# A tuned long-convolution kernel: the first convolution in nine block products instead of ten

## The chip, the cores and the metric

The kernel runs on one core of one Trainium2 chip. A core has a matrix engine (TensorE, in the profile PE, with its weight loads as PEld), VectorE (DVE), ScalarE (ACT), GpSimd (POOL) and SyncE (SP), which here issues nearly all DMAs. Each engine works through its own instructions in order; semaphores connect them. Matmul results land in PSUM, everything else lies in SBUF. The metric is device time in microseconds (us) of one execution.

## The reference, cut to what matters

There are 4 images of 64 channels, each 256 x 256, in float32. Layer 0 makes two short filters per channel (a small sine network over 256 positions, times a decay), takes their outer product as a 256 x 256 kernel and convolves each image with it causally (written with FFTs), then adds the image times a bias. Since the kernel is an outer product, it is two one-dimensional convolutions, one along each axis.

```python
hx = _implicit_filter(z, Xw1, ..., t, deltas)
hy = _implicit_filter(z, Yw1, ..., t, deltas)
k = jnp.einsum('ijk,imk->ijmk', hx, hy)[0]          # an outer product for each channel
y = jnp.fft.irfft2(u_f * k_f, s=(fft_size, fft_size))[..., :L, :L]
out = y + x * bias[:, None, None]
```

Layer 1 takes, for each image and channel, the 256 x 256 gram matrix of the rows, weighs it with a matrix of the channel, sums each row, adds that sum to the row, and normalises each channel over all images and positions.

```python
scores = jnp.einsum('bpsd,bptd->bpst', x, x) * inv_dim
red = jnp.sum(scores * weights[None], axis=-1, keepdims=True)
y = x + red
mean = jnp.mean(y, axis=(0, 2, 3), keepdims=True)
var = jnp.var(y, axis=(0, 2, 3), keepdims=True)
y_hat = (y - mean) * jax.lax.rsqrt(var + BN_EPS)
return y_hat * gamma[None, :, None, None] + beta[None, :, None, None]
```

## The kernel before, in words

The work goes channel by channel, and all four images of a channel are worked on together: two lie in the upper and lower 64 partitions (called `u`), two behind each other (called `v`). An axis of 256 is cut into 4 blocks of 64. Matmuls are 64 x 64 tiles of the array, so that four run side by side, one for each pair of `u` and `v` (the index `t` of the matmul loops).

Each channel c passes three stages on PE:

- `conv_z(c, m)` (L211), the first convolution. A causal convolution of a 256-vector is a lower triangular Toeplitz matrix, in 4 x 4 blocks of 64 with 10 that aren't zero. Block i of the input (as weights) meets the filter's columns from 64 i on, so the four matmuls are 256, 192, 128 and 64 columns wide. The Toeplitz rows lie in the tile `toep` (`hs[c]`), loaded from `g_dram` by `load_h` in four DMAs and doubled to the lower partitions by `copy_h` on ACT.
- `conv_x0(c)` (L236), the second convolution along the other axis, with the same four widths. It reads `z`, which `copy_z` on ACT has brought from PSUM (L220).
- `gram(c, v)` (L299), the gram matrix; as it is symmetric, only 10 of 16 blocks are made, in matmuls of 192 and 128 columns.

On DVE, `add_bias` (L246) brings the second convolution out of PSUM and adds the image times its bias. `weigh` (L328 `junk`, L319 `pr`) multiplies the gram blocks with the weights; row sums over the free axis come as accumulators, the rest stays as `pr`. `spread` (L340, `sp`) puts the row sums on a diagonal and adds `pr`, so that one sum over all partitions gives `red`: `all_sum` (L348), a partition all-reduce of 1024 columns on POOL. `pick_red` (L357) on ACT moves half of the result, and `add_red` (L364) on DVE adds it to the image and accumulates the sum for the mean. `sum_means` (inside `add_red`, L368) and `sum_squares` (L422) are small all-reduces on POOL; `squares` (L416) on ACT sums the squares; `root` (L428 to L432) on ACT and five small DVE operations (`newton` and `scale_shift`, L437 to L450) give the scale and shift of the channel; `finish` (L462) on ACT writes the output tile, and SP sends it out.

The order is written out by hand (`manual_schedule`): the main loop's body c runs over channels 0 to 61, and `last_channels` holds the last two. In body c, PE does conv_x0(c), then conv_z(c+1), then gram(c). DVE does add_bias(c), the small operations of channel c-3, weigh and spread of the first half of gram(c), then add_red(c-1), then weigh and spread of the second half. POOL gets all_sum(c) at the end of body c, so that its result is used in body c+1. PSUM is a pool of 8 single banks that are handed out in turn.

Of the kernel before, what the change touches and what calls it, by code (L numbers as in the profile page):

```python
# [19 lines left out]
GW = S + P // 2  # L20
COPIES = 4
H = P // 2
# [15 lines left out]
def conv_scores_bn_kernel(  # L38
# [29 lines left out]
    def load_xt(c, v, n):  # L68
        if not n:
            xts[c, v] = ld.tile([P, 4, S], F32, tag=f"xt{v}", name=f"xt_{c}_{v}", bufs=4)  # L70
        part = bass.ts(n, 2)
        nc.sync.dma_start(xts[c, v][:, part], xT[c, v, :, part])
# [39 lines left out]
    g_sb = const.tile([P, GW], F32, name="g_sb")  # L112
    nc.vector.memset(g_sb[:, S:], 0.0)

    g0_sb = const.tile([P, 2, GW], F32, name="g0_sb")
# [3 lines left out]

    g_dram = dram.tile([COPIES, C, 2, GW], F32, name="g_dram")  # L120

    hs[0] = ld.tile([P, 2, GW], F32, tag="toep", name="toep_0")
    with tc.tile_pool(name="fps", bufs=4, space=PSUM) as fps:
# [20 lines left out]
        for a in (1, 0):  # L144
# [7 lines left out]
            for n in range(2):  # L152
                row = g0_sb[H * n : H * n + 1, a, 32 * n :]
                src = bass.AP(row.tensor, row.offset, [row.ap[0], [1, 32], [1, S]])
                queue = nc.scalar if n else nc.sync
                queue.dma_start(hs[0][bass.ts(n, 32), a, :S], src)
# [5 lines left out]
        nc.vector.tensor_tensor(g_sb[:, :S], ph, decay_sb, ALU.mult)  # L162
        for a in (1, 0):
            nc.vector.tensor_copy(hs[0][H:, a, :S], hs[0][:H, a, :S])
# [4 lines left out]
    for a in (1, 0):  # L169
        queue = nc.scalar if a else nc.sync  # L170
        queue.dma_start(
            g_dram[:, :, a, :].rearrange("n c g -> c n g"),
            g_sb[bass.ts(a, C), None, :].to_broadcast([C, COPIES, GW]),
# [4 lines left out]
    def load_h(c, n):  # L178


        if not n:
            hs[c] = ld.tile([P, 2, GW], F32, tag="toep", name=f"toep_{c}")
        src = bass.AP(
            g_dram.tensor, g_dram.offset + c * 2 * GW + 16 * n,
            [[4 + C * 2 * GW, COPIES], [1, 4], [1, GW + S]],
        )
        rows = hs[c][bass.ts(n, 16)].rearrange("p a r -> p (a r)")
        nc.sync.dma_start(rows[:, : GW + S], src)

    def copy_h(c):  # L190

        toep = hs[c]
        nc.scalar.copy(toep[H:, :, :S], toep[:H, :, :S])  # L193
# [3 lines left out]
    ps = ctx.enter_context(tc.tile_pool(name="ps", bufs=8, space=PSUM))  # L197

    st8, zs = {}, {}

    def conv_z(c, m):


        toep = hs[c]
        p1 = [ps.tile([P, 2, S], F32, tag="ps", name=f"p1_{c}_{m}_{u}") for u in range(2)]
        for k in range(2):
            for i in range(4):
                for t in range(4):
# [3 lines left out]
                        p1[u][bass.ts(v, H), k, : S - H * i],  # L212
                        lhsT=xts[c, v][rows, i, bass.ts(2 * m + k, H)],
                        rhs=toep[rows, 1, H * i : S], start=(i == 0), stop=(i == 3),
# [3 lines left out]
    def copy_z(c, m, p1):  # L218
        for u in range(2):
            nc.scalar.copy(zs[c][:, u, bass.ts(m, 2), :], p1[u][:, :, ::-1])  # L220

    def conv_x0(c, z, parts=range(2)):
# [3 lines left out]
        if not c:  # L226
            first_x0(z)
            return
        for m in parts:
            p2 = [ps.tile([P, 2, S], F32, tag="ps", name=f"p2_{c}_{m}_{v}") for v in range(2)]  # L230
            for i in range(2):
                for k in range(4):
                    for t in range(4):
                        v, u = t % 2, t // 2
                        rows = bass.ts(v, H)
                        nc.tensor.matmul(  # L236
                            p2[v][bass.ts(u, H), i, : S - H * k],
                            lhsT=z[rows, u, k, bass.ts(2 * m + i, H)],
                            rhs=toep[rows, 0, H * k : S], start=(k == 0), stop=(k == 3),
                        )  # L240
            add_bias(c, m, p2)

# [539 lines left out]
```

## Time and profile before

| | |
|---|---|
| runs | 885.39, 882.55, 880.49 us |
| median | 882.55 us |
| span of the profiled execution | 872.5 us (its own device time isn't given apart from the span; the median of the runs lies 10 us above the span) |
| busy: PE, DVE, ACT, POOL | 855.9, 755.9, 621.9, 427.8 us |
| DMA | 169.69 MB, mean 194 GB/s |

The span runs from the first to the last instruction of the profiled execution. An engine's busy time counts overlapping instructions once. In the groups and windows, a mean can be longer than the distance from one start to the next, since an engine begins an instruction before the one ahead has ended. A wait is put down to what ended it.

### The profile page before, as it was taken

Reading aid. Unit: us, or ns where it says so; the run is one execution under the profiler, and the core shown is the slowest. Engines: PE = TensorE matmul, PEld = TensorE weight load, DVE = VectorE, ACT = ScalarE, POOL = GpSimd, SP = SyncE. Lnnn points to the kernel's source line nnn. Section 1 sums busy time; section 2 is a strip of 40 time slices with the busy share of each in tenths; the row PEclk is TensorE's granted clock in tenths of the full one; section 3 lists DMA queues with packets and bytes.
Section 4 is the critical chain, followed back from the end, with each engine's and each line's share of the span. In section 5 each row is a group of like instructions: output and inputs, shape, how many; then the busy total and the mean of one; then the engine's idle time right before and its main releaser. Section 6 shows DMA issues by size and latency. Waiting matters only on the chain.

```text
span 872.5 us, 55963 instructions
## 1 busy us (share of the span) xinstructions
PE 855.9 (98%) x24674; PEld 836.2 (96%) x24674; DVE 755.9 (87%) x2647; ACT 621.9 (71%) x1218; POOL 427.8 (49%) x194
## 2 busy tenths in 40 slices
PE   7999999999999999999999999999999999999995
PEld 5999999999999999999999999999999999999994
DVE  3588988988988988988998998998998988988996
ACT  2256767767767767777777777777777767767786
POOL 0236546546546546546546546546546546546530
PEclk9999999999999999999999999999999999999997
DMA  6724665565565556565565565655555655565535
GB/s 189 221 77 139 198 209 195 201 211 193 201 210 192 200 196 206 202 207 193 203 208 192 203 206 194 205 200 199 203 201 199 202 203 192 204 210 193 190 141 194
DMA packets 89870, 169.69 MB, mean 194 GB/s; under 512 B 10555, under 2 KB 11740, under 8 KB 89628
## 3 DMA queue, kind: packets, MB, share of 16 engines
q1 hardware_dynamic: 88972, 165.52, 55.6%
q8 instruction: 194, 3.18, 1.6%
q10 hardware_dynamic: 656, 0.59, 0.3%
q14 instruction: 48, 0.39, 0.2%
HBM read 98.18 MB, written 67.76 MB: 190 GB/s over the span
## 4 chain that ended last, share of the span: by engine, by line
PE 97%; DVE 2%; DMA 1%; issue 0%; ACT 0%; DVEq 0%; ACTq 0%
PE p L211 32%; PE g L299 32%; PE p L236 32%; PE p L265 0%; DMA toep<-g_sb 0%; PE ph L132 0%; DVE junk L328 0%; DMA zw_sb<-in_zw 0%; PE rp L379 0%; DVE fa L135 0%; DVE x L516 0%; DVE pr L319 0%; PE rp L384 0%; PE s L507 0%; DVE fa L140 0%
## 5 line engine op out<-in xcount | busy, mean ns | idle before, releaser
L348 POOL PARTITION_ALL_REDUCE rd<-sp x62 | 376.8, 6078 | 182.4 <-DVE sp L340 182.4
L211 PE MATMUL p<-toep,xt 64*64 64x256 f32 (+3 forms) x8192 | 304.0, 296 | 0.9 <-DMA toep<-g_sb 0.9
L299 PE MATMUL g<-x 64*64 64x192 f32 (+1 forms) x8192 | 302.5, 296 | 0.0
L211 PEld LDWEIGHTS p<-toep,xt 64*64 64x64 f32 x8192 | 291.4, 133 | 8.6 <-PE idle L168 1.5
L236 PE MATMUL p<-toep,z 64*64 64x256 f32 (+3 forms) x8064 | 298.3, 296 | 0.0
L236 PEld LDWEIGHTS p<-toep,z 64*64 64x64 f32 x8064 | 289.6, 133 | 6.8 <-issue 0.2
L299 PEld LDWEIGHTS g<-x 64*64 64x64 f32 x8192 | 289.7, 133 | 0.8 <-DVE x L246 0.2
L328 DVE SCALAR_TENSOR_TENSOR junk<-g,w 128x192 f32<-128x192 f32 x512 | 160.9, 351 | 81.1 <-PE g L299 77.7
L462 ACT ACTIVATE o<-x,sh,g 128x512 f32<-128x512 f32 x252 | 203.3, 810 | 3.0
L246 DVE SCALAR_TENSOR_TENSOR x<-xt,chan_sb,p 128x512 f32<-128x512 f32 x256 | 173.8, 739 | 7.6 <-PE p L265 7.2
L220 ACT COPY z<-p 128x512 f32<-128x512 f32 x256 | 134.7, 576 | 22.3 <-PE p L211 22.3
L416 ACT ACTIVATE sq<-x,mom 128x1024 f32<-128x1024 f32 x127 | 145.2, 1143 | 3.3 <-DVE x L405 1.1
L364 DVE SCALAR_TENSOR_TENSOR x<-x,rd 128x1024 f32<-128x1024 f32 x122 | 144.1, 1218 | 0.0
L340 DVE SCALAR_TENSOR_TENSOR sp<-eye_sb,red,pr 128x128 f32<-128x128 f32 x492 | 139.0, 344 | 0.0
L368 POOL PARTITION_ALL_REDUCE mom<-mom x61 | 24.5, 401 | 231.1 <-DVE x L364 227.1
L357 ACT COPY rd<-rd 64x512 f32<-64x512 f32 (+1 forms) x62 | 38.0, 612 | 134.8 <-POOL rd L348 134.7
L319 DVE SCALAR_TENSOR_TENSOR pr<-g,w 128x256 f32<-128x256 f32 x256 | 107.3, 419 | 0.0
L193 ACT COPY toep<-toep 64x512 f32<-64x512 f32 x63 | 38.9, 617 | 32.0 <-DMA toep<-g_dram 26.7
L411 ACT ACTIVATE mom<-mom 128x1 f32<-128x1 f32 x62 | 18.2, 293 | 38.0 <-POOL mom L368 37.1
L328 DVE DVE_READ_ACCUMULATOR junk<-g,w 128x1 f32 x512 | 42.2, 82 | 0.0
L422 POOL PARTITION_ALL_REDUCE tot<-mom x62 | 29.8, 481 | 5.1 <-ACT sq L416 5.1
L416 ACT ACTIVATION_READ_ACCUMULATOR sq<-x,mom 128x1 f32 x127 | 23.7, 186 | 0.0
(84 smaller groups left out, 220.4 us busy)
## 6 DMA issues: line engine op xcount, KB each, us to landing
xt<-in_xT SPq DMA_DIRECT2D x256, 256.0 KB
out<-o SPq DMA_DIRECT2D x256, 256.0 KB
w<-in_wl SPq DMA_DIRECT2D x64, 320.0 KB
toep<-g_dram SPq DMA_DIRECT2D x252, 36.0 KB
g_dram<-g_sb SPq DMA_DIRECT2D x1, 320.0 KB
g_dram<-g_sb ACTq DMA_DIRECT2D x1, 320.0 KB
decay_sb<-in_decay SPq DMA_DIRECT2D x1, 256.0 KB
fw_sb<-in_fw ACTq DMA_DIRECT2D x1, 192.0 KB
```

Of the source, the lines that this page charges most:

```text
L211: nc.tensor.matmul(p1[u][bass.ts(v, H), k, : S - H * i], lhsT=xts[c, v][rows, i, bass.ts(2 * m + k, H)], rhs=toep[rows, 1, H * i : S], sta ...
L220: nc.scalar.copy(zs[c][:, u, bass.ts(m, 2), :], p1[u][:, :, ::-1])
L236: nc.tensor.matmul(p2[v][bass.ts(u, H), i, : S - H * k], lhsT=z[rows, u, k, bass.ts(2 * m + i, H)], rhs=toep[rows, 0, H * k : S], start=(k ...
L246: nc.vector.scalar_tensor_tensor(st8[c][0][:, v, part], xts[c, v][:, part], chan_sb[:, 0, c : c + 1], p2[v][:, :, ::-1], ALU.mult, ALU.add,)
L299: nc.tensor.matmul(gs[u][bass.ts(h, H), o, :], lhsT=xb[rows, v, i, m, :], rhs=xb[rows, v, i, t, :], start=(i == 0), stop=(i == 3),)
L319: nc.vector.scalar_tensor_tensor(pr[:, b].rearrange("p (t s) -> p t s", s=H), g[:, COL, :], 1.0 / math.sqrt(S), w[:, 6:10, :], ALU.mult, A ...
L328: nc.vector.scalar_tensor_tensor(junk, g[:, part, :], 1.0 / math.sqrt(S), w[:, 3 * n : 3 * n + 3, :], ALU.mult, ALU.mult, accum_out=red0[: ...
L340: nc.vector.scalar_tensor_tensor(sp[:, b, part], eye_sb, red0[:, b, n : n + 1], pr[:, b, part], ALU.mult, ALU.add,)
L348: nc.gpsimd.partition_all_reduce(rd[:, part].rearrange("p b s -> p (b s)"), sp[:, part].rearrange("p b s -> p (b s)"), P, RED.add,)
L364: nc.vector.scalar_tensor_tensor(x0[:, v], x0[:, v], 1.0, rd[:, 2 * v, None, :].to_broadcast([P, 4, S]), ALU.mult, ALU.add, accum_out=mom[ ...
L416: nc.scalar.activation(sq, st8[c][0][:, v], AF.Square, bias=mom[:, 5:6], accum_out=mom[:, 6 + v : 7 + v])
L462: nc.scalar.activation(o, y, AF.Identity, bias=sh, scale=g)
```

## The change: what it does

In rows and columns of blocks, two of the ten products use the same filter block h1: one output takes h1 x1 + h0 x2 and the next h2 x1 + h1 x2, where x1 and x2 are input blocks. The changed kernel computes h1 (x1 + x2) once, and adds (h0 - h1) x2 to the one and (h2 - h1) x1 to the other. The filter differences are made once, at the start, and stored as further columns of `g_dram` (so `toep` has 832 columns instead of 576 that are loaded). The sum x1 + x2 is made by `sums(c + 2)` with two additions of 256 columns on GpSimd, two channels ahead. `conv_shared` makes the shared product with 16 matmuls of 64 columns; ACT copies it to the tile `kept`; `conv_z` makes the other eight blocks (widths 256, 2 x 64, 64, 64); `copy_z` on ACT brings the half of `z` that has no shared part, and `add_shared` on DVE adds `kept` to the other half. Channels 0, 1 and 63 keep the ten products (`conv_z_plain`).

PSUM is now handed out as four pairs of banks. Two `add_bias` of 512 columns become one of 1024 over both banks (in the main loop), and two products `pr` of 256 columns one of 512.

DVE's order in body c is now: add_bias of the first half (c,0); add_red(c-2) in two parts; add_bias(c,1); spread(c-1), eight instructions; add_shared(c+1) twice; weigh of both halves of gram(c). The five small operations of channel c-3 stand one by one between these. Body c issues all_sum(c-1) after the spreads, where body c issued all_sum(c) at its end before. ACT's and SP's orders are moved to fit.

In the order of the changed kernel's instructions, POOL has in each body: the small all-reduce of `sum_squares(c-3)`, that of `sum_means(c-2)`, an entry without operands, the two additions of `sums`, an entry without operands, and the all-reduce of `all_sum(c-1)`. The kernel before has one such entry, ahead of its first `all_sum`.

```diff
     def load_xt(c, v, n):
-        if not n:
-            xts[c, v] = ld.tile([P, 4, S], F32, tag=f"xt{v}", name=f"xt_{c}_{v}", bufs=4)
+        if c not in xts:
+            xts[c] = ld.tile([P, 2, 4, S], F32, tag="xt", name=f"xt_{c}", bufs=4)
...
+        g = g_sb[:, S:]
+        nc.vector.tensor_tensor(g[:, :S], ph, decay_sb, ALU.mult)
+        for n in range(2):
+            nc.vector.tensor_tensor(
+                g_sb[:, bass.ts(n, P)], g[:, (1 + 2 * n) * H :][:, :P], g[:, P:S], ALU.subtract
+            )
...
-        nc.scalar.copy(toep[H:, :, :S], toep[:H, :, :S])
-    ps = ctx.enter_context(tc.tile_pool(name="ps", bufs=8, space=PSUM))
+        nc.scalar.copy(toep[H:], toep[:H])
+    ps = ctx.enter_context(tc.tile_pool(name="ps", bufs=4, space=PSUM))
+    def pair_of_banks(name):
+        return ps.tile([P, 2, 2, S], F32, tag="ps", name=name)
+    def sums(c):
+        xss[c] = wk.tile([P, 2, S], F32, tag="xs", name=f"xs_{c}")
+        for v in range(2):
+            nc.gpsimd.tensor_tensor(
+                xss[c][:, v], xts[c][:, v, 1], xts[c][:, v, 2], ALU.add
+            )
+    def conv_shared(c):
+        toep = hs[c].rearrange("p (b s) -> p b s", s=H)
+        both = ps.tile([P, 2, 8, H], F32, tag="ps", name=f"shared_{c}")
+        for k in range(4):
+            for t in range(4):
+                u, v = t % 2, t // 2
+                rows = bass.ts(u, H)
+                nc.tensor.matmul(
+                    both[bass.ts(v, H), u, k], lhsT=xss[c][rows, v, bass.ts(k, H)],
+                    rhs=toep[rows, 11], start=(k == 0), stop=(k == 3),
+                )
+        kept[c] = wk.tile([P, 2, 2, P], F32, tag="kept", name=f"kept_{c}")
+        nc.scalar.copy(
+            kept[c].rearrange("p m u s -> p u m s"),
+            both[:, :, :4].rearrange("p u (m k) s -> p u m (k s)", k=2),
+        )
     def conv_z(c, m):
...
+        p1 = pair_of_banks(f"p1_{c}_{m}")
+        for k in range(2):
+            for i, (cols, outs) in enumerate((
+                (slice(9, 13), slice(0, 4)),
+                (slice(5, 13, 7), slice(0, 3, 2)),
+                (slice(7, 8), slice(1, 2)),
+                (slice(12, 13), slice(0, 1)),
+            )):
+                for t in range(4):
...
+                    nc.tensor.matmul(
+                        out[:, outs], lhsT=xts[c][rows, v, i, bass.ts(2 * m + k, H)],
+                        rhs=toep[rows, cols], start=(i == 0), stop=(i == 3),
+                    )
+        return p1
     def copy_z(c, m, p1):
-        for u in range(2):
-            nc.scalar.copy(zs[c][:, u, bass.ts(m, 2), :], p1[u][:, :, ::-1])
+        z = zs[c][:, m].rearrange("p u k s -> p (u k) s")
+        y = p1.rearrange("p u k s -> p (u k) s")
+        nc.scalar.copy(z[:, :, :P], y[:, :, : P - 1 : -1])
+    def add_shared(c, m, p1):
+        z = zs[c][:, m].rearrange("p u k (b s) -> p (u k) b s", s=H)
+        y = p1.rearrange("p u k (b s) -> p (u k) b s", s=H)
+        part = kept[c][:, m].rearrange("p u (k s) -> p (u k) s", s=H)
+        nc.vector.tensor_tensor(
+            z[:, :, :1:-1, ::-1], y[:, :, :2],
+            part[:, :, None, :].to_broadcast([P, 4, 2, H]), ALU.add,
+        )
...
+    def weigh_pair(c, v, both):
+        pr, w = st8[c][3], ws[c]
         for u in range(2):
+            weigh_rows(c, 2 * v + u, both[:, u])
+        nc.vector.scalar_tensor_tensor(
+            pr[:, 2 * v : 2 * v + 2].rearrange("p u (t s) -> p u t s", s=H), both[:, :, COL, :],
+            1.0 / math.sqrt(S), w[:, None, 6:10, :].to_broadcast([P, 2, 4, H]),
+            ALU.mult, ALU.mult,
+        )
...
     for c in range(C - 2):
         p, q, f = c - 1, c - 2, c - 3
+        short = c + 1 > 1
...
+        if c:
+            p2 = conv_x0(c, z, 0)
...
+        if c:
+            add_bias(c, 0, p2)
+        if f >= 0:
+            tot = sum_squares(f, moms[f])
+        if q >= 0:
+            pick_red(q)
+        if f >= 0:
+            scales[f] = root(f, tot)
+            steps = scale_steps(f, moms.pop(f), *scales.pop(f))
+        else:
+            steps = iter(())
+        for v in range(2):
+            if q >= 0:
+                add_red(q, v)
+            next(steps, None)
+        if q >= 0:
+            sum_means(moms[q])
+        if c + 2 < C - 1:
+            sums(c + 2)
+        if c:
+            p2 = conv_x0(c, z, 1)
...
+        if c:
+            add_bias(c, 1, p2)
+        if short:
+            conv_shared(c + 1)
+        next(steps, None)
+        for v in range(2):
+            for u in range(2):
+                if p >= 0:
+                    spread(p, 2 * v + u)
+            next(steps, None)
+        if p >= 0:
+            all_sum(p)
         if q >= 0:
             minus_mean(moms[q])
+        for m in range(2):
+            if short:
+                p1 = conv_z(c + 1, m)
+                copy_z(c + 1, m, p1)
+                add_shared(c + 1, m, p1)
...
+            if q >= 0:
+                squares(q, moms[q], m)
+        copy_h(c + 2)
...
         gram(c, 0)
-        if p >= 0:
-            moms[p] = add_red(p)
-        if c == BY_PE:
-            all_sum(c, slice(0, 2))
         gram(c, 1)
-        if c < BY_PE:
-            all_sum(c)
```

`last_channels` (c = 63) is changed to match: beside the matmuls of channel 62 it now does pick_red and add_red of channel 60, sum_squares and root of channel 59, and half of channel 61's spreads with an all_sum of half its columns; before, these stood in the last body of the main loop.

## The prediction

> **What bounds the kernel now.** I read the page's busy shares and chain first, then the windows of three channel periods, then each engine's timeline in one period, then POOL's rows.
>
> ```profile
> PE 855.9 (98%) x24674; PEld 836.2 (96%) x24674; DVE 755.9 (87%) x2647; ACT 621.9 (71%) x1218; POOL 427.8 (49%) x194
> ...
> PEclk9999999999999999999999999999999999999997
> ...
> PE 97%; DVE 2%; DMA 1%; issue 0%; ACT 0%; DVEq 0%; ACTq 0%
> ```
>
> TensorE (PE) has no idle slice and carries 97% of the chain; its granted clock falls only in the last slice, where it idles.
>
> ```profile
> 300.00:313.08 13.08, 13.08 (x391) 12.89 (x387) 11.71 (x42) 9.73 (x20) 6.92 (x3) 1.00 0.60 203
> 313.08:326.16 13.08, 13.08 (x391) 12.89 (x387) 11.71 (x42) 9.15 (x19) 6.92 (x3) 1.00 0.53 180
> ```
>
> A window's columns are length, then busy time of PE, weight loads, VectorE (DVE), ScalarE (ACT) and POOL. A channel lasts 13.08 us, all of it PE: three stages (first convolution, second convolution, gram) of 128 matmul records, 4.36 us each. DVE has 1.37 us to spare, POOL 6.16.
>
> ```profile
> 316.85 0.15 DVE L437 RECIPROCAL r<-r 128x1 f32<-128x1 f32 x1
> ...
> 319.35 0.36 DVE L328 SCALAR_TENSOR_TENSOR junk<-g,w 128x192 f32<-128x192 f32 x1 [1.16 <-PE g L299]
> ...
> 321.13 1.13 DVE L340 SCALAR_TENSOR_TENSOR sp<-eye_sb,red,pr 128x128 f32<-128x128 f32 x4
> 322.18 1.22 DVE L364 SCALAR_TENSOR_TENSOR x<-x,rd 128x1024 f32<-128x1024 f32 x1
> ```
>
> DVE's instructions overlap, so I price them from start to next start: four `sp` 1.05 us (0.262 each), `add_red` 1.147, `add_bias` of 512 columns 0.658, `pr` of 256 0.336, `junk` with its accumulator read 0.278.
>
> ```profile
> 37.42 6.12 POOL L348 PARTITION_ALL_REDUCE rd<-sp  x1 [36.99 <-DVE sp L340]
> 49.96 0.42 POOL L368 PARTITION_ALL_REDUCE mom<-mom  x1 [6.42 <-DVE x L364]
> ```
> ```profile
> L348 POOLq MODIFY_POOL_CONFIG  x2: 11/11/11, 0.8 to 0.8; - x2
> ```
>
> POOL runs one kind of instruction, partition all-reduces: 6.12, 0.48 and 0.40 us a channel. Ahead of the first, at 0.8 us, stands a pair of MODIFY_POOL_CONFIG of 11 ns; the first all-reduce follows 36.6 us later, 0.09 us after the last `sp`. Whatever that pair set going was over by then, unseen.
>
> **The change part by part.** *Matmuls.* Single records of 256, 192, 128 and 64 columns last 377, 323, 269 and 217 ns: 53.5 ns per 64 columns. Four tiles run side by side, each passing a product twice. A row of ten blocks is 2 x 10 x 53.5 = 1.07 us, four rows 4.28 (measured 4.36 with starts). Nine blocks give 4.28 x 0.9 + 0.1 = 3.96 us, counting `conv_shared`: 0.40 us less in each of 61 channels (2 to 62), 24.6 us if PE stays the bound. The load count rises from 64 to 80, and 64-column passes are shorter than the 133 ns of a weight load; but the last 64 records of L265, 128 and 64 columns in turn, start at 335 ns per sixteen, which is their streaming (2 x 160.5 ns) plus starts. So I charge nothing for loads. They are hidden by the other three tiles; a run of only 64-column passes isn't in this trace, and if each paid 133 ns (128-column ones too), the stage would grow by 1.6 us, 98 us in all. Lower end: nothing.
>
> The Trainium skill ("TensorE: Matmul & The Clock Gate", Back-to-back issue gap) puts about 25 ns under every matmul's start to start. Those 64 records start 21 ns apart, so the row is below it; by the page `conv_shared`'s 32 passes would take 0.8 us instead of 0.45, and 61 x 0.35 = 21 us of the gain would go.
>
> *VectorE.* Merged `add_bias`: 2 x (1.067 + 0.125) = 2.38 for 4 x 0.658 = 2.63. Merged `pr`: 2 x (0.533 + 0.069) = 1.20 for 1.34. Added: two `add_shared` of 512 columns from PSUM, at 0.60 (`pr`'s overhead) to 0.66 (`add_bias`'s); I take 0.60. The five small operations lose their 1.34 us chain of waits and cost five slots. A slot is what an instruction takes beyond 1.04 ns a column: 0.07 (`pr`), 0.13 (`sp`, with an operand from a tile), 0.19 if a second such operand adds as much again; say 0.5 in all. Sum: 11.92 - 0.25 - 0.14 + 1.20 - 0.84 = 11.9 us. DVE fits below 12.7.
>
> *ScalarE.* `copy_z` 2 instead of 4 (0.575 each), one `kept` 0.58, `copy_h` 832 columns instead of 512, +0.33: 0.25 us less of 9.7. Covered. *DMAs.* `load_h` grows from 36 to 52 KB, four a channel, 0.3 us more at 203 GB/s with share 0.6; the number of issues stays, and SP mostly waits for ACT's outputs. Covered. *PSUM pairs.* Seven pairs a channel over four slots; each is freed over 1 us before its reuse. Nothing.
>
> *POOL, where I put the decision.* `sums` adds two additions of 256 columns. More: the changed program's order has, on every channel, a bare entry ahead of `sums` and another ahead of `all_sum`, of the kind that stands once in the old program, where the trace has the MODIFY_POOL_CONFIG pair. There are 60 of each, and they stand exactly where POOL's kind of operation changes; so I read them as a swap of what POOL has loaded, twice a channel. I call the price of one swap r. Its lower bound is the pair's 0.02 us; its upper bound two long transfers: 9.6, since SP's next issue after the `g_dram` write stands 4.8 us behind it. Rows between (us in all, times, longest; the last by busy time and mean ns):
>
> ```profile
> PE ph L132 <- DMA zw_sb<-in_zw: 2.6, 1, 2.6
> ```
> ```profile
> SPq L188 <- DMA g_dram<-g_sb: 4.8, 2, 3.5
> ```
> ```profile
> L98 ACT ACT_TABLE_LOAD x1 | 1.3, 1283 | 1.6 <-PEq L771 1.6
> ```
>
> ACT's table swap is one record, 1.28 us. POOL's swap is two records; if what it loads comes from memory, the nearest row is the first small load, 2.6 us from the span's start to PE's first matmul. I take one for each record: r = 5.2.
>
> The swaps lie on a loop through the channels, since POOL keeps order: `sum_means(q)`, swap, `sums`, swap, `all_sum(p)`; next channel's `pick_red`, `add_red` and `sum_means` need that `all_sum`. One round: `all_sum` 6.12, `pick_red` 0.03 + 0.62, to DVE 0.05, two `add_red` and a slot 2.39, to POOL 0.17, `sum_means` 0.40, additions 1.4, two swaps. For an addition, DVE's pace (256 x 1.04 ns + 0.1) gives 0.37, the all-reduce's 5.6 ns a column 1.5; I take 0.7. Sum 11.18 + 2r = 21.6 us, 8.5 above 13.08. PE, 12.7 us of work, then waits about 9 us a channel at `gram`, which waits for `add_bias(c,1)`, queued on DVE behind `add_red(q)`. Its clock may fall in these gaps; the loop doesn't run through PE.
>
> 59 channels (2 to 60) hold both swaps: 59 x 8.5 = 502. The end moves q's spread and a half `all_sum` (3.3 us) later, beside 13 us of matmuls: 0 to 5, I take 2. The profiled execution's span is 872.5; the runs' median 882.55 lies 10 above it, which I carry as what lies around. 872.5 + 502 + 2 + 10 = 1387.
>
> The Trainium skill ("GPSIMD Engine Reference", 2.1 Instruction dispatch) says the first call after a library load pays about 6 us (5.95) that no profile row shows. By that figure the round is 23.1 us and the time an estimated 1475. The trace neither confirms nor denies it: its one swap had 36.6 us to hide in, and the first all-reduce lasted 6.12 like the others.
>
> **The rivals.** *Swaps are cheap* (r below 0.95, where the loop passes 13.08). For it: records of 11 ns; nothing ever waited for one. Against: ACT's far smaller matter costs 1.28. The next bound is DVE's loop: `add_red(q)` x2 2.29, `add_bias(c,1)` 1.19, spreads of p 7 x 0.262, 0.51 from the last one's start to POOL, 6.12, `pick_red` 0.70: 12.65, and four small slots between, 0.3 to 0.75. At 12.95, 60 x 0.13 = 8 less: 875, faster; if these overlap down to PE's 12.68, 858. This is the case on the other side.
> *Cheap swaps, slots in the middle*: 13.1 us a channel, 883 to 888, no change or just slower. The gain of nine blocks is then eaten by the order: spreads now come after `add_red` on DVE.
> *Weight loads bind*, as above: 980, only seen if swaps are cheap.
>
> **How the numbers follow.** Dear swaps 0.76; cheap and faster 0.16; cheap and within 0.5% (what a measurement here can tell from no change) 0.06; loads bind 0.02. Dear swaps alone: r from one `zw` landing (1.85 us after its issue; 14.9 us a channel, 991) to twice 3.5 (25.2, 1600). The range takes in part of the cheap cases: 870 to 1600; beyond it about 0.1 below, and 0.06 above, up to r = 9.6 (1906). Faster 0.16, same 0.06, slower 0.78.
>
> **What will show it.** Right: MODIFY_POOL_CONFIG about 240 times; POOL idle for microseconds around them with its additions or `all_sum` late; channel periods near 21 us; PE busy near 60%, waiting at `gram` for DVE; PEclk below 9 throughout. Wrong: `all_sum` starts 0.1 to 0.2 us after the last `sp`; periods near 13; then read ten or nine blocks from the first convolution's time (3.96) and DVE's loop. Most in doubt is r, which no row prices.

## The result, and the profile after

The changed kernel takes 1686.2 us (median of 4 runs, 1678.9 to 1689.7) against 881.5 us (880.2 to 885.4) of the kernel before on the same chip: 1.912 times as long, 95% interval 1.905 to 1.918. The forecast was 1387 us with a range of 870 to 1600. The side and the place were right, the size was not: the time lies 86 us above the range.

The page of the changed kernel: busy shares, the granted clock in 40 slices, the chain that ended last, and two groups on GpSimd (busy, mean ns, then the idle time before them and what ended it):

```profile
PE 993.1 (59%) x26626; PEld 851.1 (51%) x26626; DVE 800.4 (48%) x2523; ACT 602.7 (36%) x1157; POOL 515.5 (31%) x316
...
PEclk9876877778686877777687777877777787777778
...
issue 33%; POOL 26%; PE 21%; DVE 14%; ACT 3%; DMA 1%; SPq 0%; DVEq 0%; ACTq 0%; POOLq 0%
...
L439 POOL PARTITION_ALL_REDUCE rd<-sp x62 | 377.0, 6080 | 476.9 <-issue 464.4
...
L222 POOL TENSOR_TENSOR xs<-xt 128x256 f32<-128x256 f32 x122 | 86.3, 720 | 484.0 <-DVE pr L394 158.5
```

No engine is busy for even 60% of the span. A third of the chain is "issue", time in which an engine waited for nothing that the profile shows. Ahead of `all_sum` (L439) POOL loses 477 us, ahead of the additions (L222) 484. The second number is put down to DVE's `pr`, but that is a name for something that happened to end near it. PE's 21% of the chain rests mostly on the same naming, since the chain passes from the additions back to `gram`. Worked out from the records of 50 channels, the additions start between 1.0 us before and 0.9 us after the end of the nearest `gram`, so they don't wait for it.

GpSimd's timeline over one channel shows it better (start, length, operation, in brackets the idle time before):

```profile
702.62 0.40 POOL L461 PARTITION_ALL_REDUCE mom<-mom  x1 [2.87 <-DVE x L455]
711.51 1.42 POOL L222 TENSOR_TENSOR xs<-xt 128x256 f32<-128x256 f32 x2 [8.49 <-DVE junk L405]
720.19 6.13 POOL L439 PARTITION_ALL_REDUCE rd<-sp  x1 [7.27 <-issue]
726.24 0.50 POOL L512 PARTITION_ALL_REDUCE tot<-mom  x1
729.61 0.40 POOL L461 PARTITION_ALL_REDUCE mom<-mom  x1 [2.87 <-DVE x L455]
```

From `sum_means` to the additions pass 8.49 us, from the additions to `all_sum` 7.27 us. Both times POOL stands still at a change of its kind of operation, and the channel lasts 729.61 - 702.62 = 27.0 us. The additions read image blocks that had been loaded long before; `junk` and `pr` have no part in them. The instructions at these two places are the swaps (the rows of L222 and of L439: least, median and longest duration in ns):

```profile
L222 POOLq MODIFY_POOL_CONFIG  x120: 11/83/83, 0.8 to 1607.3; - x120
```
```profile
L439 POOLq MODIFY_POOL_CONFIG  x120: 1/1/15, 36.7 to 1616.8; - x120
```

That makes 240 records, none longer than 83 ns. The price is not in the record but behind it: from the first of a pair to POOL's next operation it takes 7.70 us in the median into the additions and 7.80 us into `all_sum` (worked out from the records of the trace; apart from the first, which also waits for data, single swaps lie between 5.8 and 10.3 us).

Who waits for this is in the waits (us in all, times, longest):

```profile
ACT rd L448 <- POOL rd L439: 960.2, 61, 19.0
DVE x L455 <- ACT rd L448: 740.9, 59, 14.5
...
PE g L379 <- DVE x L328: 651.8, 59, 13.4
POOL rd L439 <- issue: 464.4, 59, 9.3
```

`pick_red` waits for `all_sum`, `add_red` for `pick_red`, and PE at `gram` for the `add_bias` that is queued behind `add_red` on DVE. The window of one channel (columns as in the prediction) closes the picture:

```profile
700.00:726.70 26.70, 15.78 (x416) 13.50 (x416) 12.42 (x39) 9.12 (x18) 8.32 (x5) 0.76 0.35 101
```

DVE works 12.42 us and POOL 8.32 us of 26.7. PE takes 15.78 us for work that lasts 12.7 us at full clock (the shortest channels of a kernel below), because the clock granted is below 1 for a part of it: behind the wait for DVE, the chain has `gram`'s 128 matmuls at 7.24 us, with a granted clock of 0.63 over them, where they took 4.35 before. PE is not on the loop, so this costs nothing by itself.

### The profile page after: what moved, and what is told of

The parts are those of the page before. It is cut to its first block, busy times and chain, and to the rows that moved or that the text cites. A ratio compares the mean times of both kernels' runs of the same rounds, so it can differ in the third digit from the quotient of the medians.

```text
span 1681.8 us, 59970 instructions
## 1 busy us (share of the span) xinstructions
PE 993.1 (59%) x26626; PEld 851.1 (51%) x26626; DVE 800.4 (48%) x2523; ACT 602.7 (36%) x1157; POOL 515.5 (31%) x316
## 4 chain that ended last, share of the span: by engine, by line
issue 33%; POOL 26%; PE 21%; DVE 14%; ACT 3%; DMA 1%; SPq 0%; DVEq 0%; ACTq 0%; POOLq 0%
POOL rd L439 22%; PE g L379 19%; POOL xs L222 5%; DVE x L455 5%; DVE x L328 4%; DVE junk L405 2%; ACT rd L448 2%; DVE pr L394 1%; PE p L312 1%; DVE u L530 1%; PE p L261 0%; DMA xt<-in_xT 0%; DMA g_dram<-g_sb 0%; DMA toep<-g_dram 0%; ACT o L570 0%
## 5 line engine op out<-in xcount | busy, mean ns | idle before, releaser
L379 PE MATMUL g<-x 64*64 64x192 f32 (+1 forms) x8192 | 424.0, 381 | 652.5 <-DVE x L328 651.8
L379 PEld LDWEIGHTS g<-x 64*64 64x64 f32 x8192 | 359.5, 178 | 709.9 <-DVE x L328 659.9
L439 POOL PARTITION_ALL_REDUCE rd<-sp x62 | 377.0, 6080 | 476.9 <-issue 464.4
L261 PE MATMUL p<-toep,xt 64*64 64x64 f32 (+2 forms) x7808 | 240.2, 271 | 18.4 <-issue 18.2
L222 POOL TENSOR_TENSOR xs<-xt 128x256 f32<-128x256 f32 x122 | 86.3, 720 | 484.0 <-DVE pr L394 158.5
L261 PEld LDWEIGHTS p<-toep,xt 64*64 64x64 f32 x7808 | 203.1, 134 | 50.6 <-issue 26.6
L328 DVE SCALAR_TENSOR_TENSOR x<-xt,chan_sb,p 128x1024 f32<-128x1024 f32 x122 | 155.7, 1276 | 24.1 <-PE p L312 24.1
L394 DVE SCALAR_TENSOR_TENSOR pr<-g,w 128x512 f32<-128x512 f32 x126 | 86.4, 685 | 0.0
L276 DVE TENSOR_TENSOR z<-p,kept 128x512 f32<-128x512 f32 x122 | 78.1, 681 | 0.6 <-ACT z L270 0.6
L270 ACT COPY z<-p 128x512 f32<-128x512 f32 x122 | 69.5, 570 | 2.4 <-PE p L261 2.4
L204 ACT COPY toep<-toep 64x832 f32<-64x832 f32 x63 | 55.7, 883 | 5.5 <-DMA toep<-g_dram 4.0
```

The source lines that it names most:

```text
L222: nc.gpsimd.tensor_tensor(xss[c][:, v], xts[c][:, v, 1], xts[c][:, v, 2], ALU.add)
L261: nc.tensor.matmul(out[:, outs], lhsT=xts[c][rows, v, i, bass.ts(2 * m + k, H)], rhs=toep[rows, cols], start=(i == 0), stop=(i == 3),)
L328: nc.vector.scalar_tensor_tensor(st8[c][0][:, :, part], xts[c][:, :, part], chan_sb[:, 0, c : c + 1], p2[:, :, :, ::-1], ALU.mult, ALU.add,)
L379: nc.tensor.matmul(gs[u][bass.ts(h, H), o, :], lhsT=xb[rows, v, i, m, :], rhs=xb[rows, v, i, t, :], start=(i == 0), stop=(i == 3),)
L394: nc.vector.scalar_tensor_tensor(pr[:, 2 * v : 2 * v + 2].rearrange("p u (t s) -> p u t s", s=H), both[:, :, COL, :], 1.0 / math.sqrt(S), ...
L439: nc.gpsimd.partition_all_reduce(rd[:, part].rearrange("p b s -> p (b s)"), sp[:, part].rearrange("p b s -> p (b s)"), P, RED.add,)
```

## The experiments

The theory on trial first: each change of GpSimd between all-reduces and additions costs one swap, and the loop through `all_sum` carries two per channel. The rivals: something else of the change (the order on VectorE, the weight loads of the short matmuls, the pairs of banks) costs as much.

### The swaps alone, in the kernel before

```diff
     def all_sum(c, ...):
+        tiny = sm.tile([P, 1], F32, tag="tiny", name=f"tiny_{c}")
+        nc.gpsimd.tensor_tensor(tiny, eps, eps, ALU.add)
```

> The kernel before, with one addition of a single column on GpSimd ahead of each all_sum, and so two swaps a channel, nothing else. Theory (the price is the swap's, whatever surrounds it): swaps of 7.7 us again, on the loop all_sum 6.12, pick_red 0.65, two add_red 2.4, sum_means 0.6, two swaps and the small addition 15.7: 25.4 us a channel, about 1620 us. Rival (the swaps are slow only beside the new order and its transfers): below 1000 us.

Measured: 1564 us, ratio 1.775 (1.759 to 1.791), 3% below the 1620 expected. One addition of a single column per channel is enough. GpSimd's timeline in this kernel:

```profile
703.48 0.40 POOL L370 PARTITION_ALL_REDUCE mom<-mom  x1 [2.81 <-DVE x L366]
711.96 0.18 POOL L349 TENSOR_TENSOR tiny<-eps 128x1 f32<-128x1 f32 x1 [8.09 <-issue]
719.00 6.13 POOL L350 PARTITION_ALL_REDUCE rd<-sp  x1 [6.86 <-issue]
```

An operation of 0.18 us costs 11.4 us per channel (24.48 in the mean instead of 13.08), since 8.09 + 6.86 us of standing still come with it. Nothing else of the change is in this kernel, so the swap price is shown by itself: 7.9 us in the median into the addition, 6.4 out of it. The second is 1.3 us less than I had put in, and that makes the miss.

### Half as many swaps

The additions for two channels are made together, in every second channel.

```diff
-        if c + 2 < C - 1:
-            sums(c + 2)
+        if c % 2 == 0:
+            for n in (c + 2, c + 3):
+                if n < C - 1:
+                    sums(n)
...
-            xts[c] = ld.tile([P, 2, 4, S], F32, tag="xt", name=f"xt_{c}", bufs=4)
+            xts[c] = ld.tile([P, 2, 4, S], F32, tag="xt", name=f"xt_{c}", bufs=5)
```

> The changed kernel with sums for two channels made together in every second channel, so half the swaps (60 instead of 120); images are loaded one channel earlier, in five buffers. Theory: channels with swaps take 26.8 + 1.4 us, those without 13.1: mean 20.7, about 1340 us. Rival (the additions on GpSimd or their contention with VectorE cost, not the swaps): 1600 us or more, since as many additions are made.

Measured: 1354 us, ratio 1.536 (1.523 to 1.550), close to the 1340 expected. GpSimd's timeline:

```profile
705.43 6.13 POOL L439 PARTITION_ALL_REDUCE rd<-sp  x1 [9.01 <-issue]
...
718.57 6.12 POOL L439 PARTITION_ALL_REDUCE rd<-sp  x1 [3.32 <-DVE sp L431]
...
737.02 2.79 POOL L222 TENSOR_TENSOR xs<-xt 128x256 f32<-128x256 f32 x4 [8.33 <-PE g L379]
```

Channels with swaps last about 29 us and those without 718.57 - 705.43 = 13.14 us. The latter is VectorE's loop without swaps, which the prediction's second rival put at 13.1.

### The additions behind `all_sum`

Both swaps then lie where GpSimd would idle while `pick_red` and `add_red` run, at least in part.

```diff
-        if c + 2 < C - 1:
-            sums(c + 2)
...
         if p >= 0:
             all_sum(p)
+        if c + 2 < C - 1:
+            sums(c + 2)
```

> The changed kernel with sums issued behind all_sum(p) on POOL instead of ahead of it; as many swaps as before. Theory (a loop of latencies, not POOL's total): pick_red and add_red now run beside the swaps; what is left is POOL's own sequence, 6.13 + 0.5 + 0.4 + 1.6 + 2 x 7.7 = 24.1 us a channel, about 1540 us. Rival (only the number of swaps counts): 1686 us, as the changed kernel.

Measured: 1801 us, ratio 2.044 (2.021 to 2.067): worse than the change itself. GpSimd's timeline, and a wait of VectorE:

```profile
715.35 1.40 POOL L222 TENSOR_TENSOR xs<-xt 128x256 f32<-128x256 f32 x2 [8.84 <-issue]
722.54 0.41 POOL L512 PARTITION_ALL_REDUCE tot<-mom  x1 [5.80 <-issue]
725.10 0.40 POOL L461 PARTITION_ALL_REDUCE mom<-mom  x1 [2.16 <-DVE x L455]
728.81 6.14 POOL L439 PARTITION_ALL_REDUCE rd<-sp  x1 [3.31 <-DVE sp L431]
```
```profile
DVE r L528 <- ACT r L520: 894.9, 59, 16.7
```

I had overlooked `sum_squares`. It stands on GpSimd behind both swaps now; ACT's root waits for it, and DVE's reciprocal, which waits for the root, stands between the two `add_red` in DVE's order. So the loop still runs through both swaps and has more behind them: 28.7 us. A small operation that nobody hurries for can carry a loop, if a strict order puts an urgent one behind it.

### No swaps at all: additions left out, on VectorE, or not needed

Three kernels without any swap. The first leaves the additions out and lets the shared product read x1 alone. The second makes them on VectorE. The third keeps the changed order but makes ten products everywhere.

```diff
-        if c + 2 < C - 1:
-            sums(c + 2)
...
-                    both[bass.ts(v, H), u, k], lhsT=xss[c][rows, v, bass.ts(k, H)],
+                    both[bass.ts(v, H), u, k], lhsT=xts[c][rows, v, 1, bass.ts(k, H)],
```

> The changed kernel without the two additions on GpSimd, so without any swap; the shared product then reads block x1 alone (x2 is missing from it), all else stays. Theory (the swaps of POOL's library are nearly all of the loss, and behind them VectorE's loop is next): the loop add_red(q), add_bias(c,1), spreads(p), all_sum(p), pick_red, add_red adds up from the changed kernel's own starts to 13.1 us, so about 884 us, no gain from nine products. Rival 1 (the loop isn't the next bound): PE's 12.7 us a channel, 858 us. Rival 2 (the nine products or their weight loads are dear): 900 to 980 us.

Measured: 943.0 us, ratio 1.073 (1.068 to 1.078).

```diff
-        for v in range(2):
-            nc.gpsimd.tensor_tensor(
-                xss[c][:, v], xts[c][:, v, 1], xts[c][:, v, 2], ALU.add
-            )
+        nc.vector.tensor_tensor(
+            xss[c], xts[c][:, :, 1], xts[c][:, :, 2], ALU.add
+        )
```

> The whole change, with the sums made by one VectorE addition of 512 columns (0.61 us) at the same place in the program instead of two on GpSimd. Theory: no swap, but the addition lies inside VectorE's loop, which becomes 13.1 + 0.6 = 13.7 us: 920 us. Rival (only VectorE's total work counts, 12.1 + 0.6 = 12.7 us): 860 us.

Measured: 949.6 us, ratio 1.081 (1.074 to 1.087).

```diff
-        short = c + 1 > 1
+        short = False
```

(The last one on top of the first.)

> As e1, but all channels make ten products by the plain first convolution: PSUM in pairs and the new order of VectorE alone. Theory: the same loop of 13.1 us binds and PE needs 13.08, so 883 to 888 us, within 0.5% of e1. Rival 1 (PE binds in both): 882 here and 858 in e1, so 24 us between them.

Measured: 932.1 us, ratio 1.061 (1.055 to 1.067), from three executions; a fourth, whose profile is read below, took 939.7 us.

So the swaps explain all but some 60 us of the loss, and those 60 us are a second matter that none of my cases had. Page and PE's waits of the first kernel, and the same waits of the third:

```profile
PE 861.8 (91%) x26626; PEld 820.6 (87%) x26626; DVE 796.3 (84%) x2523; ACT 614.8 (65%) x1157; POOL 427.8 (45%) x194
```
```profile
PE p L261 <- issue: 31.9, 30, 2.3
PE g L379 <- issue: 29.9, 30, 2.0
```
```profile
PE g L379 <- issue: 28.1, 30, 2.7
PE p L291 <- issue: 11.4, 19, 1.4
```

PE stops for up to 2.7 us, 1 us in the mean, while it waits for no engine and no data that the profile names. In the kernel before, PE's waits have no such line. Worked out from the trace's records: between 60 and 820 us the first kernel has 67 such stops (75.9 us), and they lie at one fixed place in every 127.4 matmuls. The queue that the page calls "instruction" brings one packet of 16 KB per 127 matmuls, and nearly every stop ends 1.2 to 1.6 us after such a packet has ended. So PE seems to wait for its own instructions.

One more kernel changes only what VectorE waits for: spreads and `add_bias(c,1)` stand ahead of `add_red`, the addition between the two halves of `gram`, and g and sh are made on ScalarE:

```diff
+        if p >= 0:
+            for b in range(4):
+                spread(p, b)
         if c:
             p2 = conv_x0(c, z, 1)
+            add_bias(c, 1, p2)
+        if q >= 0:
+            add_red(q, 0)
...
         gram(c, 0)
+        if c + 2 < C - 1:
+            sums(c + 2)
         gram(c, 1)
...
```

> Nine products with the sums on VectorE (between the two gram halves' weighing), and VectorE's order changed once more: spreads(p) and add_bias(c,1) come before add_red(q), so that all_sum(p) no longer closes a loop within one channel; ScalarE makes the last two small operations, g and sh, and copies z before it takes the mean. Theory: no loop above 10 us is left, VectorE has 12.1 + 0.6 - 0.3 = 12.4 us of work and PE 12.7: about 859 us, 2.6% below the kernel before. Rival (VectorE's waits at 97% load reach PE): 870 to 890 us.

Measured: 951.5 us, ratio 1.084 (1.082 to 1.087). It has 88 stops, 78.4 us of PE's time between 60 and 820 us. But in this kernel VectorE covers most of them. In its new place the addition runs beside `all_sum`, and there it takes longer than in e2, where it doesn't (e2's row, then e7's: least, median and longest duration in ns):

```profile
L221 DVE TENSOR_TENSOR xs<-xt x61: 677/681/693, 28.7 to 877.3; 128x512 f32<-128x512 f32 x61
```
```profile
L221 DVE TENSOR_TENSOR xs<-xt x61: 681/2383/2498, 35.6 to 893.1; 128x512 f32<-128x512 f32 x61
```

The 55 long ones began 2.7 to 4.3 us after the start of `all_sum`, and every one ended 5.15 us after it; the four that began later than that took 0.68. So VectorE is taken not for the expected 12.4 us a channel but for 14.17, in the median from one addition to the next, and that is also what most channels last (42 of 60 take 14.1 to 14.2 us from one `all_sum` to the next). The order of VectorE has its price in the other kernels too. The shortest channels of e1 and e6 last 13.13 us from one `all_sum` to the next, as the loop of 13.1 us said, and those of e2, with the addition inside the loop, 13.73 (30 of 60). In e1, e2 and e6 the stops come on top. In time the addition costs e2 6.6 us over e1, and the ranges of the two overlap.

### Why PE stops: bursts of transfers, or more instructions

Two things differ from the kernel before that could make PE wait for its instructions. The changed order writes three of a channel's four output blocks nearly in a row and issues the loads directly behind them, so the 13 transfers of a channel are issued within 9 us, and then none for over 6 us. And a channel has 416 weight-load and matmul pairs instead of 384 (the window above says x416). First the burst, put into the kernel before:

```diff
         parts_of(c, 0)
         if c + 2 < C and c:
             load_xt(c + 2, 1, 1)
-        load_h(c + 2, 0)
-        conv_x0(c, zs.pop(c))
+        for n in range(2):
+            load_h(c + 2, n)
+        parts_of(c, 1)
+        if c + 3 < C:
+            load_xt(c + 3, 0, 0)
+        for n in range(2, 4):
+            load_h(c + 2, n)
+        parts_of(c, 2)
+        if c + 3 < C:
+            load_xt(c + 3, 1, 0)
+        load_w(c + 1)
+        if c + 3 < C:
+            load_xt(c + 3, 0, 1)
+        conv_x0(c, zs.pop(c))
...
```

> The kernel before, its computation untouched; only the places of its transfers change: ScalarE writes three of a channel's four output blocks in a row at the start of a channel, and the SyncE queue issues ten of its other transfers directly behind them, as the changed kernel does, instead of spreading them over the channel. Theory (bunched transfers delay TensorE's fetch of its own instructions): TensorE waits for nothing that the profile names at every 128th matmul, some 60 to 80 times by about 1.1 us between 60 and 820 us, and the time is about 935 us (ratio 1.06). Rival (the stalls belong to the changed order of the matmuls, or to the shorter channel): no such stalls, 875 to 886 us.

Measured: 882.0 us, ratio 1.003 (0.9996 to 1.006). A miss for the theory of bursts, but a weak one: two outputs still came 3 to 6 us apart and held the SyncE queue up. In windows of 2 us from 400 to 426 us the DMA share stayed between 0.29 and 0.86. A few stops did come in the profiled execution, which at 890.1 us is the longest of the ten:

```profile
PE p L236 <- issue: 4.5, 9, 1.2
PE g L299 <- issue: 2.5, 5, 0.9
```

The stronger test goes the other way and takes the burst out of the kernels that have it. Outputs stand about 3 to 4 us apart in ScalarE's order, each with two or three loads behind it, and the copy of the Toeplitz rows moves to the next channel's start:

```diff
+    def spaced(c, place):
+        parts_of(c, place)
+        for n in ((0,), (1,), (2, 3), ())[place]:
+            load_h(c + 2, n)
+        if c + 3 < C:
+            load_xt(c + 3, *PARTS[place])
+        if place == 3:
+            load_w(c + 1)
...
+        if c:
+            copy_h(c + 1)
+        spaced(c, 0)
...
             scales[f] = root(f, tot)
...
+        spaced(c, 1)
...
             minus_mean(moms[q])
+        spaced(c, 2)
...
+            if m:
+                spaced(c, 3)
...
```

With ten products (e6 with this edit):

> e6_ten (ten products, 384 weight-load and matmul pairs a channel as before) with its transfers spaced as in e8_spaced. Two causes of TensorE's stalls stand apart here: bunched transfers that delay its instruction fetch, and the number of its instructions. Bunching: the stalls of e6 (52 us between 60 and 820 us) are gone, 876 to 886 us. Another property of the changed order: 920 to 935 us.

Measured: 883.7 us, ratio 1.006 (1.004 to 1.009), where e6 had 1.061. The stops are gone but for two or three, and 55 of 60 channels last 13.13 us from one `all_sum` to the next, the loop through VectorE. That gives what was expected of e6 at first, 883 to 888 us. The stops that are left:

```profile
PE p L312 <- issue: 0.9, 2, 0.5
PE g L379 <- issue: 0.3, 1, 0.3
```

The windows show what was taken away. Four of e6's, then four of this kernel's, at a dense part of a channel and behind it (the last three columns are granted clock, DMA share and GB/s; the first numbers are length and PE's busy time):

```profile
406.00:408.00 2.00, 1.72 (x43) 1.51 (x46) 2.00 (x4) 0.28 (x1) 0.40 (x1) 1.00 0.85 270
408.00:410.00 2.00, 2.00 (x68) 1.90 (x64) 2.00 (x9) 1.15 (x4) 0.00 (x0) 1.00 0.88 270
410.00:412.00 2.00, 2.00 (x65) 1.93 (x60) 1.03 (x5) 2.00 (x5) 0.99 (x1) 1.00 0.43 162
412.00:414.00 2.00, 2.00 (x68) 2.00 (x61) 0.56 (x5) 1.98 (x4) 2.00 (x1) 1.00 0.00 0
```
```profile
404.00:406.00 2.00, 2.00 (x64) 1.87 (x60) 1.74 (x9) 1.51 (x2) 2.00 (x1) 1.00 0.84 275
406.00:408.00 2.00, 2.00 (x67) 1.87 (x63) 1.55 (x3) 0.88 (x2) 1.46 (x2) 1.00 0.61 210
408.00:410.00 2.00, 2.00 (x65) 1.87 (x60) 2.00 (x4) 1.22 (x4) 0.00 (x0) 1.00 0.44 158
410.00:412.00 2.00, 2.00 (x66) 1.90 (x62) 2.00 (x7) 1.18 (x4) 0.40 (x1) 1.00 0.50 168
```

In e6 PE is idle in the first of them, at a DMA share of 0.85, and from 412 to 414 us nothing is moved; with the transfers spaced the share stays at 0.44 or more, and PE has no idle time. The share of one window doesn't decide, though: e6 has no idle time at 0.88, and this kernel none at 0.84. What goes with the stops is when the instruction packet comes. Worked out from the records between 60 and 820 us, from PE's first pair of one packet to the end of the next packet pass 2.9 us in the median in e6 and 2.2 here, and the slowest tenth takes more than 4.1 and 2.9 us; PE goes on into a packet's pairs only 1 us or more after its end. The 127 pairs last about 4.36 us in both. So in e6 the packets come later, and often too late. The same bytes, products and engines: the spacing is worth some 48 us, by the two ratios.

With nine products (e1 and e7 with this edit):

> e1_no_sums, still without the additions (the shared product reads one image block alone, so the computation is not the reference's), with its transfers spaced as before: ScalarE's four output blocks stand 3 to 4 us apart in its order, each with two to four loads behind it on the SyncE queue, and the copy of the Toeplitz rows moves to the start of the next channel. Theory: the 67 stalls of e1 (75.9 us between 60 and 820 us) shrink to under 15 us, and the time goes from 943 to about 870 us (VectorE's loop of 13.1 us by 59 channels and 98 us for the ends give 871). Rival (the stalls have another cause): 930 to 945 us.

Measured: 906.8 us, ratio 1.028 (1.024 to 1.032), where e1 had 1.073. Spacing gives back 36 us, but not the 73 I expected. The shortest channels (15 of 60) last 13.13 us, VectorE's loop, as expected; the mean is 13.7, and what lies between is stops.

> e7_order (whole computation, the addition on VectorE, its order such that the wait for the all-reduce is covered) with the transfers spaced as in e8_spaced. Theory: the 88 stalls of e7 (78.4 us) shrink to under 15 us; VectorE's own work of 13.0 us a channel by 59 and 98 us for the ends give 865 us, ratio about 0.985. Rival (the stalls have another cause): 940 to 955 us.

Measured: 943.7 us, ratio 1.072 (1.069 to 1.074), where e7 had 1.084. Most of the loss stays, but not because of the stops. DVE is busy for 96% of the span, and the addition beside `all_sum` again lasts 2.49 us in the median. Two of them on DVE, and the `all_sum` beside which the second began on GpSimd:

```profile
401.65 2.49 DVE L221 TENSOR_TENSOR xs<-xt 128x512 f32<-128x512 f32 x1
...
415.82 2.48 DVE L221 TENSOR_TENSOR xs<-xt 128x512 f32<-128x512 f32 x1
```
```profile
413.15 6.20 POOL L438 PARTITION_ALL_REDUCE rd<-sp  x1
```

The addition ends at 418.30, again 5.15 us after the start of `all_sum`. From one addition to the next DVE has no gap, and that takes 415.82 - 401.65 = 14.17 us; 58 of 60 channels last between 14.1 and 14.2 us. So VectorE, with the long addition in its row, sets the pace here, and PE's stops (30 us in its waits) are covered. With 14.17 instead of 13.0 us the expectation's own sum gives 59 x 14.17 + 98 = 934 us. As a test of the spacing e9 therefore says little. Nine products with spaced transfers and the addition at a place without `all_sum` weren't run.

What is left of e8 is the other difference, the number of instructions. It can be had without anything else of the change, by splitting the 192-column matmuls of the kernel before:

```diff
-                    nc.tensor.matmul(
-                        p1[u][bass.ts(v, H), k, : S - H * i],
-                        lhsT=xts[c, v][rows, i, bass.ts(2 * m + k, H)],
-                        rhs=toep[rows, 1, H * i : S], start=(i == 0), stop=(i == 3),
-                    )
+                    for a, b in ((0, 96), (96, 192)) if i == 1 else ((0, S - H * i),):
+                        nc.tensor.matmul(
+                            p1[u][bass.ts(v, H), k, a:b],
+                            lhsT=xts[c, v][rows, i, bass.ts(2 * m + k, H)],
+                            rhs=toep[rows, 1, H * i + a : H * i + b],
+                            start=(i == 0), stop=(i == 3),
+                        )
```

> The kernel before, where each matmul of 192 columns of the first convolution is split into two of 96: the same columns and the same result, but 416 weight-load and matmul pairs a channel instead of 384, as the nine products have. Its transfers stay spaced. Number of instructions as a cause (a fetch of 128 pairs needs some 4.2 us from one to the next: e8_spaced, 13.69 us a channel by 3.25 fetches): stalls appear and a channel takes about 13.5 us instead of 13.08, 900 us (ratio 1.025). Bunching alone as a cause: no stalls, 876 to 886 us.

Measured: 907.9 us, ratio 1.033 (1.030 to 1.036). The instruction queue's line on the page of the kernel before, and on this kernel's (packets, MB, share of the DMA engines):

```profile
q8 instruction: 194, 3.18, 1.6%
```
```profile
q8 instruction: 210, 3.44, 1.7%
```

The stretch from 100 to 800 us, in the kernel before and in this one:

```profile
100.00:800.00 700.00, 700.00 (x20553) 689.56 (x20549) 627.16 (x2194) 520.37 (x1019) 368.29 (x161) 1.00 0.59 201
```
```profile
100.00:800.00 700.00, 692.60 (x21437) 665.61 (x21433) 603.16 (x2113) 504.04 (x978) 355.92 (x156) 1.00 0.59 194
```

In the same time this kernel issues 21437 matmuls instead of 20553, 4.3% more, where its channel needs 8.3% more. Its channels last 13.57 us on average; the shortest, with no stop, 13.10. So the halves themselves cost 0.02 us, and the rest is PE waiting. The pace is about the same as in e8: 13.57 / 3.25 = 4.18 us per 128 pairs here, 13.69 / 3.25 = 4.21 there. The kernel before needs 13.08 / 3 = 4.36, so a packet may come later there before PE feels it. That about 4.2 us is a fixed limit of the supply isn't shown: the channels of 13.10 us get 128 pairs in 4.03, and the time to the end of the next packet, counted as above, varies from packet to packet (2.5 us in the median in this kernel, over 3.1 in the slowest tenth).

No kernel here beats the one before; e11 comes closest, at 1.006. Nine products at 384 pairs or fewer weren't tried, since I found no way to write them.

## Why the prediction was right or wrong

**The mechanism: right.** Two swaps per channel lie on the loop that it named, and the chain, the waits and e3 show it. Four of the five signs under "Right" came: 240 MODIFY_POOL_CONFIG, POOL standing idle around them, PE at 59% waiting at `gram` for DVE, and a clock below 9 nearly throughout. The fifth failed: of the periods it said "near 21"; they are 26.8.

**The size of r: the step that failed.** "I take one for each record: r = 5.2" priced a swap by the first small load, 2.6 us for each record. Measured: 7.70 us into the additions, 7.80 into `all_sum`. With this the prediction's own sum holds: 11.18 + 7.70 + 7.80 = 26.7 us, against a measured mean of 26.8; 59 x (26.7 - 13.08) = 804, and with 2, 10 and 872.5 it makes 1688, against 1686. The other terms of the loop were good: from the start of `all_sum` to that of `sum_means` the sum has 9.38 us, the lines above 729.61 - 720.19 = 9.42, and an addition was taken as 0.7 and lasts 0.72. The nearest row was a transfer, not a swap, and a choice near the middle of bounds of 0.02 and 9.6 was no measurement. The range should have followed the upper bound, but it stopped at r = 7.0, a second transfer's length.

**The page's figure.** The Trainium skill ("GPSIMD Engine Reference", 2.1 Instruction dispatch) says 5.95 us for the first call after a library load; from it the prediction estimated 1475 us. That was the better of the two numbers and still too low by 1.8 us a swap. That the time shows in no profile row, as the page says, agrees with these records of at most 83 ns. Here it is paid at every change, back and forth.

**Matmuls: right in size, wrong in worth.** The prediction put nine blocks at 3.96 us and charged nothing for weight loads. A channel of e8 without a stop, from PE's timeline (first records of the shared product, of the other eight blocks, and of the gram):

```profile
405.40 0.22 PE L235 MATMUL shared<-toep,xt 64*64 64x64 f32 x1
...
405.87 0.38 PE L261 MATMUL p<-toep,xt 64*64 64x256 f32 x1
...
409.40 0.33 PE L379 MATMUL g<-x 64*64 64x192 f32 x1
```

The stage lasts 409.40 - 405.40 = 4.00 us, 0.47 of it for the 32 passes of `conv_shared`: 15 ns from one to the next. The 25 ns of the Trainium skill ("TensorE: Matmul & The Clock Gate", Back-to-back issue gap) would make this an estimated 0.8; the trace decides for the streaming time. But it isn't the load that binds, nor the columns: 128 pairs of these short passes are through in some 3.2 us, and the next packet of instructions often comes later than that. The 0.36 us that nine products save came through in no kernel here: at 416 pairs a channel PE stops (e8, e12), and VectorE's loop lets no channel of the main loop of e1, e6, e8 or e11 last less than 13.13 us. The rival "weight loads bind", at 980 us, was looking in the right stage for the wrong resource: e1's 943 us could have been taken for it, and only the 4.00 us of an undisturbed stage excludes it.

**"DMAs: Covered": wrong.** I counted bytes and issues and found them unchanged, and didn't look at when they are issued. The order alone, with ten products and no swaps, costs 6% (e6), and all but 0.6% comes back when the transfers are spaced (e11). In the changed kernel this is hidden behind the swaps: its "issue" waits at the first convolution are 18.2 us in all, beside 651.8 at `gram`.

**VectorE: right.** From start to next start, a merged `add_bias` takes 1.19 us and `add_shared` 0.60, as predicted; the loop without swaps was given as 13.1 in the second rival, e5 has 13.14, and e11 13.13. With swaps and bursts gone, e11 at 883.7 us is what that rival said, 883 to 888.

**The rival on the other side: wrong.** "Swaps are cheap" promised 858 to 875 us. With no swaps at all, the changed order takes 943 (e1), slower by 7%. The 0.16 that I gave to "faster" stood on a next bound that was not the next one: between the swaps and DVE's loop lay the bursts and the instruction supply. And the loop itself came out at 13.13 us, not at the 12.95 or less that a gain needed.

## What to carry to other kernels

Look at the kind of an operation that is added to GpSimd, before its length: 1.4 us of additions cost two swaps of 7.8 us per channel, and even one column costs two swaps. When PE is at 98%, count its instructions as well as its columns; a rewrite that saves columns with shorter matmuls can run into the supply of instructions: here 8% more pairs for the same columns cost 3%. When work moves from one engine to another, look at what runs beside it: the addition took 0.68 us on VectorE in one place and 2.49 beside `all_sum`. And when an order is rewritten, draw when each transfer is issued, not only how many bytes there are: bunched transfers cost some 48 us here, and the waits name none of them.

## What the hardware showed that I had not expected

- A swap on GpSimd costs 6 to 10 us, in both directions, with records of 1 to 83 ns. The price isn't constant: 7.9 and 6.4 us in the median in e3, 8.84 and 5.80 in the lines of e4.
- PE stops for its own instructions. They come in packets of 16 KB per 127 matmuls, and the page counts them on the same 16 DMA engines as the data. When a packet comes too late, because transfers are bunched or because 127 pairs are through sooner, PE stands still for up to 2.7 us. That the late packet is the cause is argued from where the stops lie, from when they end, and from the packets coming later in e6 (2.9 us) than in e11 (2.2); that the spacing of transfers and the number of pairs each bring the stops about is shown (e11 against e6, e12 against the kernel before).
- An addition on VectorE with both inputs in SBUF that began beside the all-reduce of `all_sum` (2.7 to 4.3 us after its start) ended 5.15 us after that start, in 55 cases in e7 and 59 in e9; elsewhere it lasts 0.68 us. Why isn't shown.
- The profile has no name for this wait. It appears as "issue", and part of it, in stops under 0.3 us, in no wait at all: e12's list has only 10.4 us of its 28.
